# Attention of a macaron block: exponentials times values as seven block products instead of eight

## The chip, the cores and the metric

The kernel runs on one core of a Trainium2 chip. The metric is the device time of one execution in microseconds (us), as the median of several runs. The engines of the core work in parallel, each with its own queue of instructions: TensorE (PE in the profile; its weight loads are PEld), VectorE (DVE), ScalarE (ACT), GpSimd (POOL), and SyncE (SP), which issues transfers. An engine carries out its queue in order; an instruction that needs another engine's result waits for it, and everything behind it on that engine waits too.

## The reference

The input x has 4 batches of 512 rows and 256 columns, in float32. Three steps follow each other, each on the layernormed x and added to x:

```python
x = x + 0.5 * _L0_ffn_ref(_layernorm(x), ...)
x = x + _L0_attn_ref(_layernorm(x), Wq, Wk, Wv, fc_w, fc_b)
x = x + 0.5 * _L0_ffn_ref(_layernorm(x), ...)      # the same weights
```

The feed-forward part has one shared expert and 16 routed experts, of which each row uses the two with the highest scores. The attention has three heads, each 256 wide:

```python
scores = jnp.einsum('bne,hde->hbnd', x, Wq) ... * scale      # Q K^T
w = jax.nn.softmax(scores, axis=2)            # over the query rows
attn = jnp.einsum('hbnm,hbmd->hbnd', w, V)
return jnp.mean(attn, axis=0) @ fc_w.T + fc_b
```

The softmax runs over the rows n of the queries, so its sum z belongs to a key m and can be moved into the values: V[m] is scaled by 1/z[m]. The mean over heads and the output matrix are folded into the value weights, so the result of attention is the sum over three heads of (exponentials, 512x512) times (values, 512x256).

## The kernel before

**Layout.** A batch of x is a tile xs[b] of 128 partitions x 4 row tiles (index j) x 256 columns. The exponentials es[h] lie with the key on the partitions, as 128 x 4 key tiles (m) x 512 queries; the values vs[h] as 128 x 4 key tiles (m) x 256. All of this is float32, and each float32 matmul shows in the trace as two pairs of a weight load and a matmul.

**One batch of attention** (the loop at L844). GpSimd forms four sums of quarters of the transposed rows (S1 to S4, L855 to L858). query(h) multiplies the rows by a folded matrix on PE (py, 128x512, L868) and ScalarE copies the result to y (L872). quadrants(h) computes the 512x512 scores of a head from seven products of blocks: GpSimd forms the right sums T1 to T4 (L881 to L884), PE multiplies (psc, L896), and ScalarE (L910, L912), GpSimd (L913) and VectorE (L911 to L920) add the parts into ex; VectorE finds the maxima (nmax, L903) and ScalarE takes the exponentials in place (L905), with their sums z. After three heads GpSimd adds the bias to x (L950). value(h) (L924 to L938) multiplies the rows by the folded value weights (pv, L929), and the result is scaled by 1/z on its way out of PSUM: by VectorE for head 1 (L934), by ScalarE for the others (L938). Then the next batch's rows are normalized and transposed (layernorm_T, L261 to L294). The last step is the one that changes: for each row tile j, 12 matmuls over three heads and four key tiles sum into one PSUM bank pa (L970), 256 columns wide, and VectorE adds the bank to x (L975).

**What runs beside it.** For b > 0, the second feed-forward part of the batch before is prepared between the transposes and the products: PE computes the router's scores psr (L335), ScalarE a sigmoid (L353), and then router (L359 to L445) is a chain of small VectorE operations: key (L384), and twice a maximum, comparisons and a mask "one" (L388 to L392), the first followed by L394. PE counts ranks from the masks (psk, L400, in two groups, one after each mask), and the chain goes on on VectorE up to L433. Then GpSimd issues eight indirect transfers (L438), which scatter rows, with their weights in an extra column, to a table in device memory, sorted by expert. After batch 3 and its router, the tail is a series: table, loads, and the routed experts (L628 to L671), whose rows return to x at the very end.

**Order.** A planner lays the instructions of each engine in an order from the program order and its own costs and due times; a few groups of PE and ScalarE are ordered by hand with in_turn (L814 to L825, L990, L1046), none of them within the batch loop. At the start of batch 2, ffn.more() (L708 to L711) puts a branch that every engine passes; PE then waits for VectorE's queue to have passed it. Pools of tiles set limits as well: PSUM banks come from the tags mm and dn (three each), rt and rk (one each). In SBUF, "ey" has eight buffers, "h" and "g" two each, "xt" three. The tag ey is used by T1, T2 and T4; g by S1 to S4.

Of the kernel before, what the change touches and what calls it, by code (L numbers as in the profile page):

```python
# [10 lines left out]
F32 = mybir.dt.float32  # L11
# [4 lines left out]
ALU = mybir.AluOpType  # L16
AX = mybir.AxisListType
P = 128
# [3 lines left out]
def tile_macaron_block(  # L22
# [33 lines left out]
    nc = tc.nc  # L56
    B, N, H = x.shape
    NH = Wq.shape[0]
    NE = gate_w.shape[1]
    F = shared_gate_w.shape[1]  # L60
    NJ = N // P
# [37 lines left out]
    work = ctx.enter_context(tc.tile_pool(name="work", bufs=2))  # L99
    att = ctx.enter_context(tc.tile_pool(name="att", bufs=2))  # L100
    dram = ctx.enter_context(tc.tile_pool(name="dram", bufs=1, space=bass.MemoryType.DRAM))
    psum = ctx.enter_context(tc.tile_pool(name="psum", bufs=3, space=bass.MemoryType.PSUM))
# [25 lines left out]
    xs = []  # L128
# [113 lines left out]
    def moments(b, n, on_act=False):  # L242

        mv = small.tile([P, NJ, 2], F32, tag="mv", name=f"mv_{n}")
        for j in range(NJ):
            st = small.tile([P, 6], F32, tag="st", name=f"st_{n}_{j}")
            nc.vector.bn_stats(out=st, in_=xs[b][:, j, :])
            nc.vector.bn_aggr(out=mv[:, j, :], in_=st)
        std = small.tile([P, NJ], F32, tag="std", name=f"std_{n}")
        rooted[n] = mark(f"root {n}", nc.scalar.activation(std, mv[:, :, 1], AF.Sqrt, bias=eps))  # L250
        rstd = small.tile([P, NJ], F32, tag="rstd", name=f"rstd_{n}")
        last = nc.vector.reciprocal(rstd, std)
        off = None
        if on_act:
            off = small.tile([P, NJ], F32, tag="off", name=f"off_{n}")
            last = nc.vector.scalar_tensor_tensor(
                off, mv[:, :, 0], -1.0, rstd, ALU.mult, ALU.mult
            )
        return mv, rstd, off, last

    def layernorm_T(b, which, dispatch=False, moms=None):  # L261

        n = f"{which}_{b}"
        mv, rstd, off, _ = moms or moments(b, n)

        pts = [psum.tile([P, N], F32, tag="dn", name=f"pt_{n}_{c}") for c in range(NC)]
        rows = (
            partial(att.tile, tag="y", bufs=4) if n in ("ln0_2", "ln0_3")
            else partial(work.tile, tag="xn", bufs=4)
        )  # L270
        xn = [rows([P, NJ, W], F32, name=f"xn_{n}_{k}") for k in range(NK if dispatch else 1)]
        for j in range(NJ):
            if off is not None and n != "ln0_1":
                mark(f"norm {n}", nc.scalar.activation(
                    xn[0][:, j, 0:H], xs[b][:, j, :], AF.Identity,
                    bias=off[:, j : j + 1], scale=rstd[:, j : j + 1],
                ))
            else:
                normed[n] = nc.vector.tensor_scalar(
                    xn[0][:, j, 0:H], xs[b][:, j, :], mv[:, j, 0:1], rstd[:, j : j + 1],  # L280
                    ALU.subtract, ALU.mult,
                )
            for c in range(NC):
                mark(f"T{n}", nc.tensor.transpose(  # L284
                    pts[c][:, j * P : (j + 1) * P], xn[0][:, j, c * P : (c + 1) * P], ident
                ))
        xnT = acts.tile([P, NC, N], F32, tag=f"xnT{b}", name=f"xnT_{n}")
        ins = mark(f"copy {n}", nc.scalar.copy(xnT[:, 0, :], pts[0]))
        if off is not None or n == "ln0_0":
            ins = mark(f"copy {n}", nc.scalar.copy(xnT[:, 1, :], pts[1]))  # L290
        else:
            nc.vector.tensor_copy(xnT[:, 1, :], pts[1])  # L292
        copied[n] = ins
        return xnT, xn  # L294
# [443 lines left out]
    m = [moments(0, "ln0_0")]  # L738
# [105 lines left out]
    for b in range(B):  # L844
# [6 lines left out]
        halves = [slice(0, N // 2), slice(N // 2, N)]  # L851
# [9 lines left out]
        ys, es, rzs, vs = {}, {}, {}, {}  # L861
# [62 lines left out]
        def value(h):  # L924
            v = vs[h] = att.tile([P, NJ, H], F32, tag="y", name=f"v_{b}_{h}", bufs=4)
            for m in range(NJ):
                pv = psum.tile([P, H], F32, tag="mm", name=f"pv_{b}_{h}_{m}")
                for c in range(NC):
                    nc.tensor.matmul(  # L929
                        pv, xnT[:, c, m * P : (m + 1) * P], G[h][:, c, :],  # L930
                        start=(c == 0), stop=(c == NC - 1),
                    )
                if h == 1:
                    nc.vector.tensor_scalar(  # L934
                        v[:, m, :], pv, rzs[h][:, m : m + 1], None, ALU.mult
                    )
                else:
                    nc.scalar.mul(v[:, m, :], pv, rzs[h][:, m : m + 1])  # L938
# [9 lines left out]
        quadrants(1)  # L948
        quadrants(2)
        nc.gpsimd.tensor_tensor(xs[b], xs[b], fcb4, ALU.add)  # L950
        for h in range(NH):
            value(h)
        if b + 1 < B:
            ffn.add(b + 1)
            att_xnT[b + 1], _ = layernorm_T(b + 1, "lna")
        if b > 0:
# [4 lines left out]
            if b == B - 1:  # L961
# [1 line left out]
                ffn2.early()  # L963
                ffn2.loads()
                ffn2.empty()
        for j in range(NJ):
            pa = psum.tile([P, H], F32, tag="mm", name=f"pa_{b}_{j}")
            for h in range(NH):
                for m in range(NJ):
                    nc.tensor.matmul(  # L970
                        pa, es[h][:, m, j * P : (j + 1) * P], vs[h][:, m, :],
                        start=(h == 0 and m == 0), stop=(h == NH - 1 and m == NJ - 1),
                    )
            xj = xs[b][:, j, :]
            nc.vector.tensor_tensor(xj, xj, pa, ALU.add)  # L975


    ffn2.scores(B - 1)
# [55 lines left out]
    halves = [slice(j, j + 2) for j in range(0, NJ, 2)]  # L1034
# [44 lines left out]
```

## Time and profile before

| What | Value |
|---|---|
| Median of 3 runs | 508.78 us (508.70 to 510.14) |
| Profiled execution: its time | 540.54 us |
| Profiled execution: its span | 538.7 us |
| Attention of batches 1, 2, 3 in the trace | 220.97 to 286.61, to 352.13, to 416.00 |
| PE busy in the span | 484.5 us (90%) |
| Products exponentials x values on PE | 384 matmuls of 128x256 |
| Adds of the products to x on VectorE (L975) | 16, of 0.42 us |
| Indirect scatters of the routers on GpSimd (L438) | 64, of 0.98 us |

The profiled execution is longer than the median of the runs; durations and sums below are of this one execution. A row of the groups reads: line, engine, operation, output <- inputs, shape, count, then total busy time and mean nanoseconds of one, then the idle time of the engine just before such instructions and what ended most of it. In the timeline each line is the start, the duration, the engine, the line and the operation; a bracket holds the idle time before it and what released it. In the chain in order of time each line is a start, a duration, an engine, the tile and the line: it follows the work that ended last. "PEclk" or the granted clock is TensorE's clock as a share of full speed.

### The profile page before, as it was taken

The numbers are of one execution on the slowest core, as the hardware profiler recorded it, in microseconds if no ns is written. First come the engines' busy times: TensorE is split into PE (matmuls) and PEld (weight loads), VectorE is DVE, ScalarE is ACT, GpSimd is POOL, SyncE is SP. The second block draws the span as 40 slices with busy tenths as digits, with TensorE's granted clock in tenths as the row PEclk, the third lists the DMA queues.
The fourth block names the chain that finished last, engine by engine and source line by source line (L and its number), as shares of the span: only waits on it lengthen the run. The fifth ranks groups of instructions, "written<-read, shape, count | busy, mean of one in ns | idle before, by whom it ended". The sixth has DMA issues, their size and how long they took to land. (4 is left out here: it accounts for less than half of the span.)

```text
span 538.7 us, 7948 instructions
## 1 busy us (share of the span) xinstructions
PE 484.5 (90%) x2262; PEld 374.9 (70%) x2262; DVE 295.4 (55%) x981; ACT 224.6 (42%) x514; POOL 234.7 (44%) x281
## 2 busy tenths in 40 slices
PE   8977249999999899999999999999999767999984
PEld 4666037888656788678885778867888445788852
DVE  6834345555787771258325883336753642555565
ACT  3743015666543770255402664054630313466630
POOL 2466714665658321242254512553014174355653
PEclk9877769999999999999999999999999886999998
DMA  7993364557420000000012000200002245255856
GB/s 266 357 370 125 118 226 122 164 161 230 170 89 1 2 0 1 0 0 2 2 69 89 0 2 0 79 2 1 1 11 99 64 171 178 90 165 179 273 177 208
DMA packets 34734, 57.39 MB, mean 107 GB/s; under 512 B 4928, under 2 KB 25408, under 8 KB 34688
## 3 DMA queue, kind: packets, MB, share of 16 engines
q1 hardware_dynamic: 25424, 32.99, 19.7%
q0 software_dynamic: 8160, 23.44, 12.0%
q10 hardware_dynamic: 1104, 0.42, 0.3%
q8 instruction: 20, 0.33, 0.3%
q14 instruction: 26, 0.21, 0.1%
HBM read 30.78 MB, written 26.05 MB: 105 GB/s over the span
## 5 line engine op out<-in xcount | busy, mean ns | idle before, releaser
L671 POOL DMA_INDIRECT y_d<-ey,to x82 | 80.0, 976 | 66.5 <-ACT xt L632 45.8
L438 POOL DMA_INDIRECT xn_d<-xn_ln,pos x64 | 62.5, 977 | 91.7 <-DVE fa L489 23.0
L644 PE MATMUL peg<-gu,xt 128*128 x328 | 87.5, 391 | 1.9 <-DVE g L597 1.6
L970 PE MATMUL pa<-v,ex 128*128 128x256 f32 x384 | 86.2, 382 | 0.0
L970 PEld LDWEIGHTS pa<-v,ex 128*128 128x128 f32 x384 | 71.6, 190 | 9.2
L644 PEld LDWEIGHTS peg<-gu,xt 128*128 128x128 f32 x328 | 57.6, 195 | 9.0 <-issue 1.7
L661 DVE COPY hT<-pht 128x128 f32<-128x128 f32 x82 | 23.8, 291 | 60.1 <-issue 28.6
L666 PE MATMUL pey<-dn,hT 128*128 x164 | 50.4, 390 | 5.6 <-DVE hT L661 4.6
L670 ACT ACTIVATE ey<-pey,xg 128x256 f32<-128x256 f32 x82 | 38.9, 474 | 28.0 <-issue 15.7
L929 PE MATMUL pv<-G,xnT_lna 128*128 128x256 f32 x192 | 43.5, 382 | 2.7 <-ACT v L938 2.1
L868 PE MATMUL py<-xnT_lna,A 128*128 128x512 f32 x96 | 42.7, 593 | 1.0 <-DVEq L710 1.0
L929 PEld LDWEIGHTS pv<-G,xnT_lna 128*128 128x128 f32 x192 | 36.0, 190 | 9.6 <-ACT v L938 3.3
L905 ACT ACTIVATE ex<-ex,nmax 128x512 f32<-128x512 f32 x48 | 34.2, 714 | 18.6 <-DVE nmax L903 18.4
L650 ACT ACTIVATE sig<-peg 128x128 f32<-128x128 f32 x82 | 22.8, 278 | 42.7 <-PE peg L644 27.3
L632 ACT COPY xt<-pxt 128x256 f32<-128x256 f32 x82 | 29.8, 366 | 14.6 <-PE pxt L628 8.4
L605 PE MATMUL po<-sd,h 128*128 128x256 f32 x64 | 17.1, 415 | 19.1 <-DVE h L598 17.7
L975 DVE TENSOR_TENSOR x<-x,pa 128x256 f32<-128x256 f32 x16 | 6.7, 420 | 50.1 <-PE pa L970 41.3
L666 PEld LDWEIGHTS pey<-dn,hT 128*128 128x128 f32 x164 | 25.2, 194 | 12.4 <-issue 5.1
L628 PE MATMUL pxt<-ident,xg 128*128 128x128 f32 x164 | 32.3, 279 | 0.9 <-DVE xnT_ln L292 0.8
L872 ACT COPY y<-py 128x512 f32<-128x512 f32 x24 | 13.8, 581 | 46.1 <-PE py L868 46.0
L868 PEld LDWEIGHTS py<-xnT_lna,A 128*128 128x128 f32 x96 | 18.2, 190 | 20.6 <-issue 19.8
L881 POOL TENSOR_TENSOR right<-y 128x256 f32<-128x256 f32 x12 | 9.3, 775 | 50.0 <-ACT y L872 50.0
(201 smaller groups left out, 876.0 us busy)
## 6 DMA issues: line engine op xcount, KB each, us to landing
xg<-xn_d SPq DMA_DIRECT2D x82, 129.0 KB
gu<-ffn_experts_gate_up_dram SPq DMA_DIRECT2D x4, 1024.0 KB
yg<-y_d SPq DMA_DIRECT2D x8, 512.0 KB
y<-y_d SPq DMA_DIRECT2D x6, 512.0 KB
dn<-_L_ffn_experts_down_dram SPq DMA_DIRECT2D x2, 1024.0 KB
x<-in_L_attn_x_dram SPq DMA_DIRECT2D x3, 512.0 KB
out_dram<-x SPq DMA_DIRECT2D x3, 512.0 KB
y_d<-ey,to POOLq DMA_INDIRECT x82
```

Of the source, the lines that this page charges most:

```text
L438: ins = nc.gpsimd.indirect_dma_start(out=self.xn_v[k * NT + b * NJ + j], out_offset=bass.IndirectOffsetOnAxis(ap=pos[:, k, j : j + 1], axi ...
L628: ins = nc.tensor.transpose(pt[:, c, :], xg[:, c * P : (c + 1) * P], ident)
L632: nc.scalar.copy(xt, pt)
L644: nc.tensor.matmul(pg, xt[:, c, :], gu[:, bass.ds(e, 1), c, :], start=(c == 0), stop=(c == NC - 1),)
L661: self.flips.append(nc.vector.tensor_copy(hT, pt))
L666: self.downed = nc.tensor.matmul(py, hT, dn[:, bass.ds(e, 1), :], start=True, stop=True)
L670: nc.scalar.mul(y, py, xg[:, H + 1 : W])
L671: ins = nc.gpsimd.indirect_dma_start(out=self.y_v[i], out_offset=bass.IndirectOffsetOnAxis(ap=tos[i], axis=0), in_=y, in_offset=None,)
L868: nc.tensor.matmul(py, A[h][:, c, fc * P : (fc + 1) * P], xnT[:, c, :], start=(c == 0), stop=(c == NC - 1),)
L905: nc.scalar.activation(ex[:, m, :], ex[:, m, :], AF.Exp, bias=nmax[:, m : m + 1], accum_out=z[:, m : m + 1],)
L929: nc.tensor.matmul(pv, xnT[:, c, m * P : (m + 1) * P], G[h][:, c, :], start=(c == 0), stop=(c == NC - 1),)
L970: nc.tensor.matmul(pa, es[h][:, m, j * P : (j + 1) * P], vs[h][:, m, :], start=(h == 0 and m == 0), stop=(h == NH - 1 and m == NJ - 1),)
```

## The change

The exponentials and the values of each head are cut into 2x2 blocks: E11, E21, E12, E22 are halves of the keys (two m each) by halves of the queries, V11, V12, V21, V22 halves of the keys by halves of the columns. The four blocks of the result, x11 to x22, are then formed from seven products of blocks instead of eight. A product is a sum over three heads and two key tiles for two row tiles, in one PSUM bank of 128 x 2 x 128; its matmuls are 128 columns wide.

- GpSimd forms, per head, R1 = E21 + E22 in a new tile (tags h, h and g) and E21 = E11 - E21 in place, 128x512 each.
- VectorE forms, per head, W1 = V12 - V11 and W2 = V22 - W1 in new tiles (tag ey) and V12 = V22 - V12 in place, 128x256 each.
- Between the products VectorE updates the blocks in place: E11 = R1 - E11 after product 1, E12 = E12 - E11 and V21 = W2 - V21 after product 2, each per head.
- The results are added to x part by part. ScalarE copies product 1 to u; VectorE adds products to x11, u, w, x22, x12 and x21; GpSimd adds u to x12 and w to x21 and x22.
- The four matmul groups at L970 and the four adds at L975 are removed.

In the order that the planner makes of it, head 0's two GpSimd sums come among the T sums of head 2, ahead of L913 of head 1; those of heads 1 and 2 come after the last L913. VectorE's updates stand between the router's steps of the same phase. GpSimd's additions of w to x21 and x22 come behind the eight scatters L438 of that phase in batches 1 to 3.

```diff
         quadrants(2)
         nc.gpsimd.tensor_tensor(xs[b], xs[b], fcb4, ALU.add)
+        cols = [slice(0, P), slice(P, H)]
+        E11, E21, E12, E22 = (
+            [es[h][:, m : m + 2, n] for h in range(NH)] for m in (0, 2) for n in halves
+        )
+        R1 = [
+            work.tile([P, 2, N // 2], F32, tag="hhg"[h], name=f"r1_{b}_{h}") for h in range(NH)
+        ]
+        for h in range(NH):
+            nc.gpsimd.tensor_tensor(R1[h], E21[h], E22[h], ALU.add)
+            nc.gpsimd.tensor_tensor(E21[h], E11[h], E21[h], ALU.subtract)
+        V11, V12, V21, V22, W1, W2 = ([] for _ in range(6))
         for h in range(NH):
             value(h)
+            for part, (m, f) in zip((V11, V12, V21, V22), ((m, f) for m in (0, 2) for f in cols)):
+                part.append(vs[h][:, m : m + 2, f])
+            for part in (W1, W2):
+                part.append(work.tile(
+                    [P, 2, P], F32, tag="ey", name=f"w_{b}_{h}_{len(part)}", bufs=8
+                ))
+            nc.vector.tensor_tensor(W1[h], V12[h], V11[h], ALU.subtract)
+            nc.vector.tensor_tensor(W2[h], V22[h], W1[h], ALU.subtract)
+            nc.vector.tensor_tensor(V12[h], V22[h], V12[h], ALU.subtract)
...
-        for j in range(NJ):
-            pa = psum.tile([P, H], F32, tag="mm", name=f"pa_{b}_{j}")
-            for h in range(NH):
-                for m in range(NJ):
-                    nc.tensor.matmul(
-                        pa, es[h][:, m, j * P : (j + 1) * P], vs[h][:, m, :],
-                        start=(h == 0 and m == 0), stop=(h == NH - 1 and m == NJ - 1),
-                    )
-            xj = xs[b][:, j, :]
-            nc.vector.tensor_tensor(xj, xj, pa, ALU.add)
+        x11, x12, x21, x22 = (xs[b][:, j : j + 2, f] for j in (0, 2) for f in cols)
+        def summed(i, lhs, rhs):
+            pa = psum.tile([P, 2, P], F32, tag="mm", name=f"pa_{b}_{i}")
+            for j in range(2):
+                for h in range(NH):
+                    for m in range(2):
+                        nc.tensor.matmul(
+                            pa[:, j, :], lhs[h][:, m, j * P : (j + 1) * P], rhs[h][:, m, :],
+                            start=(h == 0 and m == 0), stop=(h == NH - 1 and m == 1),
+                        )
+            return pa
+        u, w = (work.tile([P, 2, P], F32, tag="xt", name=f"uw_{b}_{i}", bufs=3) for i in range(2))
+        p1 = summed(1, E11, V11)
+        nc.scalar.copy(u, p1)
+        nc.vector.tensor_tensor(x11, x11, p1, ALU.add)
+        for h in range(NH):
+            nc.vector.tensor_tensor(E11[h], R1[h], E11[h], ALU.subtract)
+        p2 = summed(2, E12, V21)
+        nc.vector.tensor_tensor(x11, x11, p2, ALU.add)
+        for h in range(NH):
+            nc.vector.tensor_tensor(E12[h], E12[h], E11[h], ALU.subtract)
+            nc.vector.tensor_tensor(V21[h], W2[h], V21[h], ALU.subtract)
+        p6 = summed(6, E11, W2)
+        nc.vector.tensor_tensor(u, u, p6, ALU.add)
+        p7 = summed(7, E21, V12)
+        nc.vector.tensor_tensor(w, u, p7, ALU.add)
+        nc.gpsimd.tensor_tensor(x12, x12, u, ALU.add)
+        p5 = summed(5, R1, W1)
+        nc.vector.tensor_tensor(x22, x22, p5, ALU.add)
+        nc.vector.tensor_tensor(x12, x12, p5, ALU.add)
+        nc.gpsimd.tensor_tensor(x21, x21, w, ALU.add)
+        nc.gpsimd.tensor_tensor(x22, x22, w, ALU.add)
+        p4 = summed(4, E22, V21)
+        nc.vector.tensor_tensor(x21, x21, p4, ALU.subtract)
+        p3 = summed(3, E12, V22)
+        nc.vector.tensor_tensor(x12, x12, p3, ALU.add)
```

## The prediction

> **What bounds the kernel now.** I read busy shares, a windows view cut at the batches' borders, groups, the chain in order of time, and the timeline around batch 1's products, in that order.
>
> ```profile
> PE 484.5 (90%) x2262; PEld 374.9 (70%) x2262; DVE 295.4 (55%) x981; ACT 224.6 (42%) x514; POOL 234.7 (44%) x281
> ```
>
> TensorE has work for 90% of the span. By stage (start:end, length, busy time of PE, PEld, DVE, ACT, POOL, then the granted clock):
>
> ```profile
> core 0: us, PE busy (x) PEld busy (x) DVE busy (x) ACT busy (x) POOL busy (x), PEclk, DMA share, GB/s
> 220.97:286.61 65.64, 63.98 (x295) 51.49 (x294) 31.12 (x68) 24.49 (x51) 23.02 (x27) 1.00 0.06 21
> 286.61:352.13 65.52, 64.46 (x293) 51.48 (x294) 39.42 (x94) 27.00 (x54) 26.27 (x32) 1.00 0.08 29
> 352.13:416.00 63.87, 63.21 (x290) 50.79 (x289) 35.13 (x96) 26.17 (x52) 20.48 (x25) 1.00 0.06 20
> 437.50:447.40 9.90, 3.92 (x11) 2.14 (x11) 1.00 (x5) 1.12 (x3) 6.13 (x7) 0.61 0.65 254
> 447.40:456.00 8.60, 8.60 (x30) 6.69 (x31) 3.05 (x15) 3.92 (x12) 3.86 (x4) 0.66 0.43 125
> ```
>
> The first three rows are attention of batches 1 to 3: PE fills them to 97-99% at full clock, the other engines have half of the time free. So cutting PE's work could pay there 1:1, and any new wait of PE costs 1:1. The last two rows are the entry to the routed experts: PE idles, and the next stretch still has clock 0.66.
>
> ```profile
> L970 PE MATMUL pa<-v,ex 128*128 128x256 f32 x384 | 86.2, 382 | 0.0
> ...
> L913 POOL TENSOR_TENSOR ex<-ex 128x512 f32<-128x512 f32 x12 | 15.2, 1270 | 11.4 <-ACT ex L912 11.4
> ```
>
> The products to be changed are 384 instruction pairs, 96 per batch. A mean of 382 overlaps its neighbours, so I take the pitch from the chain below: 68 pairs in 14.76 us, 217 ns each, 20.8 us a batch. The chain, batch 2:
>
> ```profile
> 309.19 1.23 POOL ex L913
> ...
> 310.44 0.70 DVE ex L915
> ...
> 337.33 14.76 PE pa L970 x68
> ```
>
> Before the values, the chain leaves PE for GpSimd's add L913 and a run of VectorE steps to the last exponential; lateness on GpSimd there is lateness of PE. After it the products run unbroken. Batch 1's end, timeline:
>
> ```profile
> 265.94 0.23 DVE L384 TENSOR_TENSOR key<-s,bias_bc 128x64 f32<-128x64 f32 x1 [2.19 <-ACT s L353]
> ...
> 267.23 0.23 DVE L392 TENSOR_TENSOR one<-rev,first 128x64 bf16<-128x64 f32 x1
> ...
> 281.43 0.97 POOL L438 DMA_INDIRECT xn_d<-xn_ln,pos  x1 [0.30 <-issue]
> ...
> 285.58 0.42 DVE L975 TENSOR_TENSOR x<-x,pa 128x256 f32<-128x256 f32 x1 [4.76 <-PE psk L400]
> ...
> 286.61 0.67 PE L868 MATMUL py<-xnT_lna,A 128*128 128x512 f32 x1 [1.01 <-DVEq L710]
> ```
>
> Three things run beside the products: the router's chain on VectorE (L384 to L433), eight row scatters on GpSimd (272.46 to 282.40, pitch 1.28), and the adds L975. Nothing after L975 waits for the scatters now. Batch 2's first query matmul waits for VectorE's queue to pass the branch at L710.
>
> **TensorE.** Removed per batch: 96 pairs at 256 columns. Added: 7 x 2 x 3 x 2 x 2 = 168 pairs at 128 columns. Near rows: transposes with 128 columns, 8 in 0.87 us = 109 ns; psr (16 columns, the same weights) 14 in 1.47 = 105. I take 110: 18.5 us against 20.8, -2.35 per batch, -9.4 in all. Break-even is 124 ns. Against this speaks the Trainium skill ("TensorE: Matmul & The Clock Gate", section "Back-to-back issue gap"): sustained weight-load-and-matmul pairs of 128 columns take some 81 ns where the isolated matmul takes 56, because the weight load shares the budget. That ratio, 1.46, on my 110 gives an estimate of 160 ns, 26.9 us a batch, +24 over four. The transposes alternate both operands too and stay at 109, so I keep 110; 160 is the upper end.
>
> **Sums ahead of the products.** GpSimd gets six 128x512 sums per batch, 6 x 1.27 = 7.6 us. By the changed program's order, head 0's second sum stands ahead of L913 of head 1, so that L913, VectorE's chain, the values and PE come 1.25 later. The rest lies behind the last L913, under values and transposes. VectorE gets nine 128x256 operations (0.42 each, L975); three stand before the evictions L934 that PE's value banks wait for: +0.5, in batch 0 up to +1.0. Together about +1.75 (b0 +2.2). An operation delayed[...] is seen once (an L732 add of 1024 columns took 2.19 instead of 1.45), but L913 runs beside VectorE's maxima unslowed: 0 to +1 a batch, I take 0.2.
>
> **VectorE among the products.** Removed: four L975 adds (1.7). Added: nine 128x512 updates in place (0.70, L915) and eight half-size adds to x, u, w (0.42 each): 6.3 + 3.4 = 9.7. They stand between the router's steps in VectorE's queue. The first needs product 1, and key (L384) stands behind two of them. Batch 1, with the phase 1.75 later: the router's scores (psr) end at 267.25 instead of 265.5; each product is 24 pairs, 2.64 us, and product 1 ends near 268.8, since some of its pairs fill gaps between the transposes and scores as the pairs do now; two updates, then key ends 269.8 (was 266.2). Until the first "one" mask there are then x11, a third update, E12 of head 0 and V21 of head 0 (2.5 us): 273.4 (was 267.5). PE's rank matmuls (L400) wait for it within product 6, a stall of 1.4. Up to the second mask lie x11, the other four updates and u: 278.0 (was 270.4), a stall of 1.3 within product 7. Product 7 ends at 279.8, and 5, 4, 3 end at 282.45, 285.1, 287.7. PE alone ends so 2.2 later than now: the saving is spent on the stalls.
>
> **GpSimd's queue.** The pair of adds x21+=w, x22+=w stands behind the eight scatters in GpSimd's order. The scatters start after the router's tail: 272.46 + 7.6 = 280.05, last end 290.0. Then x21+=w to 291.0 (0.73 by the 128x256 rows of L881-L884). VectorE's x21-=p4 must follow it, x12+=p3 comes behind that: 291.9. Queued behind these on VectorE is the branch L710, so py starts at 292.5 instead of 286.61: **+5.9**, with PE idle for 4.8. Batch 0 has no router in its products: +2.2 - 2.35 = **-0.1**. Batch 2: the same gate; x21-=p4 holds the bank of product 4, which the second query tile of batch 3 needs: 358.9 instead of 352.97, **+5.9**, and +0.5 because the fetch of the next rows and GpSimd's next sums come behind it. Batch 3: scatters 411 to 421.2, x21 at 421.95, x22 at 422.7; x12+=p3 and then four row statistics of x (one remained before) to the root at 424.95 against 417.12: +7.8, and +0.5 for the second router's start behind it: **+8.3**. The tail (norm, scores, scatters, experts) is serial after it and takes it 1:1.
>
> **Clock.** The trace has PE busy 3.92 of 9.90 at 437.5, then 0.61 and 0.66. The Trainium skill (same page, "The HAM clock gate") says that idleness throttles the array and that some us of work release it. By the rows alone, an idle time of 5 to 8 us costs nothing beyond itself or up to 8.60 x 0.34 = 2.9; three gaps, 0 to 8.7. I take 2.5 in all: only 4.8 us are empty in the first gap, and the third runs into a serial tail, where the clock matters little.
>
> **Sum.** -0.1 + 5.9 + 6.4 + 8.3 + 2.5 = +23.0, on the profiled execution's 540.54 (span 538.7). The runs' median, 508.78, is 6% under it, though the attention part has clock 1.00 in the profile; waits for GpSimd don't scale with TensorE's clock. I take +22: 508.8 + 22 = **531**.
>
> **Rivals.**
> A. *The gate is weak*: scatters overlap, VectorE catches up, and only the insertion on GpSimd and the rank stalls count, about +2 to +3 per batch: 508.8 + 10 = 519. For it: x21+=w itself needs only product 7. Against it: the queue order is fixed.
> B. *PE is the bound and the rest is hidden* (the other side): below 124 ns a pair, with no wait for the scatters: -9.4 gives 499.4; with the delay ahead of the values (3 x 1.75 + 2.2 = 7.45) it is 506.8, still faster. It decides only if the scatters end before product 4 does (285.1), so if they start 5 us sooner than I work out. For it: 97-99% of PE. Against it: scatters ended at 282.4 even before, and the router is now behind 9 us of updates.
> C. *No net change*: B's gain meets A's costs: 508.8.
> D. *Narrow pairs are dear*: 160 ns adds 24 on PE; longer products hide about half of the gate, +35: 544. Serial (load and stream one after the other, 216) would give about 577. Against it: 109 in the transposes.
>
> **How the numbers follow.** Chances: main case 0.72, A 0.10, B 0.07, C 0.03, D 0.08. The main case's own range: the gates' sum 20.5 less 4 (the router's delay over-counted by 1.3 a batch) gives 525; clock and port at their upper ends, +8.7 + 4 - 3, give 540. The range reaches to A's middle below and D's estimate above: 515 to 545, with some 0.08 below and 0.06 above it. About 0.3% is what a measurement of this kernel can tell from no change. Faster by more: B, and a little of A, 0.08. Within: 0.03. Slower: 0.89.
>
> **What would show it.** Right: 168 pairs at about 110 ns where unbroken; L913 of head 1 later by 1.25; the first mask 4 to 6 us later against the scores; scatters right ahead of x21+=w on GpSimd; the query of batch 2 released by VectorE's queue, with 4 to 6 us of idle PE; the last statistics held by GpSimd's x22. Wrong: if scatters start soon after the scores (VectorE takes router steps between the updates without waiting), the gate shrinks; if pairs take over 124 ns, PE is the bound and slower; if GpSimd's adds slow down beside VectorE's updates, the sum is too small.

## The result

The changed kernel takes 528.26 us (median of 4 runs, 527.37 to 528.58) against 509.46 for the kernel before: 1.0356 times as long, 95% interval 1.0327 to 1.0385, that is 3.6% or some 18.8 us slower. The forecast was 531, or +22.

The first part of the page of the changed kernel, to be set against the row shown of before:

```profile
PE 482.5 (92%) x2549; PEld 377.8 (72%) x2550; DVE 336.0 (64%) x1069; ACT 225.4 (43%) x518; POOL 274.9 (52%) x317
```

TensorE has 287 instructions more; VectorE has 41 us more work, GpSimd 40 us more. This profiled execution took 528.58 (span 526.8), close to its median, while the first profiled execution of the kernel before had been 540.54. Busy times of TensorE from the two are not comparable, so the kernel before was profiled once more:

> The kernel before, unchanged, for a second profiled execution. The first one was 540.5 against a median of 508.8. If the attention part is stable, batch 1 to batch 2 and batch 2 to batch 3 take 65.6 and 65.5 again from first query to first query, and the 30 us lie in the two feed-forward parts; if not, the stage sums of my comparison are off by what differs.

It took 509.02 (span 507.2), with this row:

```profile
PE 475.9 (94%) x2261; PEld 370.6 (73%) x2262; DVE 294.5 (58%) x981; ACT 224.5 (44%) x514; POOL 234.3 (46%) x281
```

Against it TensorE is busy for 6.6 us more after the change, not for less. Its windows, batch by batch from the first query matmul to the next one, then to the reciprocal L252 of batch 3's norm, then to the first scatter of the last router (columns as in the windows shown of before):

```profile
135.66:200.73 65.07, 62.90 (x269) 49.89 (x268) 38.48 (x74) 26.89 (x52) 24.23 (x25) 1.00 0.02 7
200.73:266.37 65.64, 63.98 (x296) 51.49 (x294) 31.12 (x68) 24.50 (x51) 22.97 (x27) 1.00 0.06 19
266.37:331.67 65.30, 64.24 (x293) 51.28 (x293) 39.38 (x93) 26.99 (x54) 26.51 (x32) 1.00 0.08 31
331.67:397.19 65.52, 64.86 (x294) 51.36 (x292) 36.14 (x99) 26.49 (x54) 20.44 (x25) 1.00 0.07 23
397.19:407.91 10.72, 7.68 (x50) 5.34 (x49) 6.91 (x31) 4.65 (x9) 0.00 (x1) 1.00 0.30 76
```

Batches 1 and 2 take 65.64 and 65.30, as in the first profile (65.64 and 65.52). Nearly all of the 31.5 us between the two executions lie in the feed-forward parts: attention began at 155.9 there and begins at 135.7 here, and the part after the last router's first scatter is 10 us shorter here. The same windows of the changed kernel:

```profile
135.88:201.58 65.70, 61.74 (x341) 50.27 (x340) 49.67 (x90) 25.86 (x52) 34.31 (x33) 1.00 0.02 7
201.58:271.56 69.98, 63.52 (x368) 51.88 (x367) 42.74 (x96) 25.90 (x53) 32.30 (x37) 1.00 0.05 16
271.56:338.75 67.19, 65.01 (x364) 52.41 (x365) 47.09 (x108) 26.09 (x54) 32.70 (x35) 0.98 0.08 27
338.75:411.94 73.19, 64.94 (x367) 51.54 (x365) 46.86 (x128) 28.38 (x56) 34.82 (x41) 0.99 0.07 23
411.94:426.85 14.91, 12.48 (x49) 9.11 (x49) 7.01 (x31) 4.38 (x8) 0.00 (x0) 0.57 0.27 71
```

| Stage | Before (second profile) | After | Difference | Forecast |
|---|---|---|---|---|
| Batch 0 | 65.07 | 65.70 | +0.6 | -0.1 |
| Batch 1 | 65.64 | 69.98 | +4.3 | +5.9 |
| Batch 2 | 65.30 | 67.19 | +1.9 | } +14.7 |
| Batch 3, to L252 | 65.52 | 73.19 | +7.7 | } for both |
| L252 to the last router's first scatter | 10.72 | 14.91 | +4.2 | clock, +2.5 for all gaps |
| Rest (to the span's end) | 99.3 | 99.95 | +0.7 | 0 |
| Sum | | | +19.4 | +23.0 |

In the first two rows of after PE is busy for up to 1.2 us less than before, and in batch 1 it stands idle for 6.5 us instead of 1.7. In the last row the granted clock is 0.57, and PE is busy for 12.48 us with the work that took 7.68 before: 4.8 of the 6.6 us are this stretch.

**The gate.** The end of batch 1 in the timeline of the changed kernel:

```profile
258.89 2.84 PE L997 MATMUL pa<-w,r 128*128 128x128 f32 x24
...
259.37 1.00 POOL L438 DMA_INDIRECT xn_d<-xn_ln,pos  x1 [1.58 <-DVE xn_ln L433]
...
261.57 5.52 PE L997 MATMUL pa<-v,ex 128*128 128x128 f32 x48
...
268.33 0.97 POOL L438 DMA_INDIRECT xn_d<-xn_ln,pos  x1 [0.30 <-issue]
269.32 0.73 POOL L1022 TENSOR_TENSOR x<-x,uw 128x256 f32<-128x256 f32 x1
...
270.09 0.42 DVE L1025 TENSOR_TENSOR x<-x,pa 128x256 f32<-128x256 f32 x1 [7.57 <-POOL x L1022]
...
271.56 1.19 PE L868 MATMUL py<-xnT_lna,A 128*128 128x512 f32 x1 [4.42 <-DVEq L710]
```

Read it from the end. The query waits 4.42 us for VectorE's queue; VectorE stood 7.57 us in L1025 for GpSimd's L1022; L1022 starts as soon as the eighth scatter has been issued. PE had finished product 3 by 267.1. This wait of TensorE for GpSimd's queue, by way of VectorE's, is called the gate below. The first two PE lines also price the narrow pair: 24 pairs from 258.89 to 261.57, 111.7 ns each.

**Ahead of the values.** GpSimd and VectorE in the middle of batch 1:

```profile
220.53 1.31 POOL L961 TENSOR_TENSOR r<-ex 128x512 f32<-128x512 f32 x1 [6.78 <-ACT ex L905]
221.79 0.73 POOL L881 TENSOR_TENSOR right<-y 128x256 f32<-128x256 f32 x1
...
222.48 1.27 POOL L962 TENSOR_TENSOR ex<-ex 128x512 f32<-128x512 f32 x1
...
225.76 1.26 POOL L913 TENSOR_TENSOR ex<-ex 128x512 f32<-128x512 f32 x1
227.05 0.69 DVE L915 TENSOR_TENSOR ex<-ex,psc 128x512 f32<-128x512 f32 x1 [3.64 <-POOL ex L913]
```

Both sums of head 0 (L961, L962) stand ahead of L913 of head 1, not one. L913 starts 24.18 after the batch's first query; in the second profile of the kernel before it starts at 222.44, 21.71 after it. VectorE waits 3.64 for it. The scatters begin at 259.37, 57.79 after the first query, instead of 51.49.

### The profile page after: what moved, and what is told of

Its sections match the earlier page's. It is cut to its first block, busy times and chain, and to the rows that moved or that the text cites. A ratio compares the mean times of both kernels' runs of the same rounds, so it can differ in the third digit from the quotient of the medians.

```text
span 526.8 us, 8711 instructions
## 1 busy us (share of the span) xinstructions
PE 482.5 (92%) x2549; PEld 377.8 (72%) x2550; DVE 336.0 (64%) x1069; ACT 225.4 (43%) x518; POOL 274.9 (52%) x317
## 5 line engine op out<-in xcount | busy, mean ns | idle before, releaser
L438 POOL DMA_INDIRECT xn_d<-xn_ln,pos x64 | 62.3, 974 | 54.4 <-DVE held L459 17.1
L997 PE MATMUL pa<-v,ex 128*128 128x128 f32 x480 | 57.9, 277 | 0.0
L997 PEld LDWEIGHTS pa<-v,ex 128*128 128x128 f32 x480 | 55.5, 192 | 0.1
L666 PE MATMUL pey<-dn,hT 128*128 x164 | 49.3, 383 | 1.4 <-DVE hT L661 1.4
L868 PE MATMUL py<-xnT_lna,A 128*128 128x512 f32 x96 | 44.5, 611 | 6.1 <-DVEq L710 4.4
L929 PE MATMUL pv<-G,xnT_lna 128*128 128x256 f32 x192 | 45.1, 385 | 3.9 <-ACT v L938 2.3
L872 ACT COPY y<-py 128x512 f32<-128x512 f32 x24 | 13.7, 579 | 80.1 <-PE py L868 80.1
L961 POOL TENSOR_TENSOR r<-ex 128x512 f32<-128x512 f32 x12 | 15.6, 1302 | 56.7 <-ACT ex L905 56.7
L868 PEld LDWEIGHTS py<-xnT_lna,A 128*128 128x128 f32 x96 | 18.6, 197 | 26.8 <-issue 23.1
L628 PEld LDWEIGHTS pxt<-ident,xg 128*128 128x128 f32 x164 | 22.9, 144 | 12.8 <-DMA xg<-xn_d 2.0
L903 DVE TENSOR_REDUCE nmax<-ex 128x2 f32<-128x1024 f32 x24 | 29.1, 1213 | 0.1
## 6 DMA issues: line engine op xcount, KB each, us to landing
gu<-ffn_experts_gate_up_dram SPq DMA_DIRECT2D x4, 1024.0 KB, 14.7
```

The costliest lines, as they stand in the source:

```text
L438: ins = nc.gpsimd.indirect_dma_start(out=self.xn_v[k * NT + b * NJ + j], out_offset=bass.IndirectOffsetOnAxis(ap=pos[:, k, j : j + 1], axi ...
L628: ins = nc.tensor.transpose(pt[:, c, :], xg[:, c * P : (c + 1) * P], ident)
L666: self.downed = nc.tensor.matmul(py, hT, dn[:, bass.ds(e, 1), :], start=True, stop=True)
L868: nc.tensor.matmul(py, A[h][:, c, fc * P : (fc + 1) * P], xnT[:, c, :], start=(c == 0), stop=(c == NC - 1),)
L903: nc.vector.tensor_reduce(nmax[:, ms], ex[:, ms, :], AX.X, ALU.max, negate=True)
L929: nc.tensor.matmul(pv, xnT[:, c, m * P : (m + 1) * P], G[h][:, c, :], start=(c == 0), stop=(c == NC - 1),)
```

## Experiments

My theory: the change pays 2 us a batch on TensorE and loses it by three separate waits, (a) GpSimd's sums ahead of L913, (b) the router delayed on VectorE, (c) the additions of w behind the scatters, and by the half clock that follows the gaps (the stretches of granted clock near 0.5). Rivals: narrow pairs are dear; or the additional work as such fills the engines, so that no single wait matters. All ratios are to the kernel before; the changed kernel stands at 1.0356.

### The narrow pair alone

```diff
-            for h in range(NH):
-                for m in range(NJ):
-                    nc.tensor.matmul(
-                        pa, es[h][:, m, j * P : (j + 1) * P], vs[h][:, m, :],
...
+            for f in (slice(0, P), slice(P, H)):
+                for h in range(NH):
+                    for m in range(NJ):
+                        nc.tensor.matmul(
+                            pa[:, f], es[h][:, m, j * P : (j + 1) * P], vs[h][:, m, f],
```

> The kernel before with its eight block products, each row tile's group cut into two column halves: 192 pairs of 128 columns per batch instead of 96 of 256, nothing else. If a 128-column pair takes the 111.5 ns that 24 of them take in the changed kernel (2.68 us from product 5 to product 4), the products take 21.4 us a batch instead of 20.8: +0.6 a batch, about +2.3 in all, 511 to 512. If narrow pairs were dear in this place (rival D, 160 ns), 30.7 us a batch and about 548.

Measured: 513.38, ratio 1.0045 (1.0019 to 1.0072), some 2.3 us. Narrow pairs cost what the changed kernel's own trace says; rival D is out. The change's 168 pairs at 111.7 ns take 18.8 us, so 2.1 less than 96 wide ones.

### The additions of w on VectorE

```diff
-        nc.gpsimd.tensor_tensor(x21, x21, w, ALU.add)
-        nc.gpsimd.tensor_tensor(x22, x22, w, ALU.add)
+        nc.vector.tensor_tensor(x21, x21, w, ALU.add)
+        nc.vector.tensor_tensor(x22, x22, w, ALU.add)
```

> The changed kernel with its two additions of w to x21 and x22 on VectorE instead of GpSimd, so that nothing of x stands behind the scatters. My theory (the gate): the idle 4.4 us of TensorE before batch 2 fall to 1, batch 3's second query tile no longer waits (2.7), batch 3's statistics come 3 earlier, and the half clock after these gaps goes (1.6 and about 3): about -12, so 516, range 513 to 519. Rival A (lateness ahead of the values and of the router is what counts): under -4, so 525 or more.

Measured: 523.94, ratio 1.0234 (1.0190 to 1.0279). The gain is real (the interval does not touch the changed kernel's), but the time lies between the two expectations. Batch 1 takes 66.98 instead of 69.98, as the theory has it. Batch 2 shows where the rest went, timeline of this run:

```profile
269.56 0.97 POOL L438 DMA_INDIRECT xn_d<-xn_ln,pos  x1 [0.30 <-issue]
269.76 7.11 PE L868 MATMUL py<-xnT_lna,A 128*128 128x512 f32 x16 [1.40 <-DVEq L710]
...
273.39 0.80 SPq L720 DMA_DIRECT2D yg<-y_d  x2
...
277.10 2.89 DVE L732 TENSOR_TENSOR x<-x,yg 128x1024 f32<-128x1024 f32 x2 [8.33 <-DMA yg<-y_d]
...
283.44 3.70 PE L868 MATMUL py<-xnT_lna,A 128*128 128x512 f32 x8 [0.53 <-DVE ex L911]
```

PE starts batch 2 at once, but the scatters are still late, and by the code the fetch of the next batch's rows takes buffers of the tag xn, from which the scatters read: it is issued 3.6 after the first query (in the first profile of before at 284.93, 1.7 ahead of it). The rows are then added and normalized by VectorE in front of batch 2's score additions. So batch 2 takes 68.53 instead of 67.19: the lateness of the scatters has a second way to PE. The tail's half clock stayed too: the 12 us from 408 on have a mean granted clock of 0.57.

### GpSimd's sums behind the last L913

```diff
-            nc.gpsimd.tensor_tensor(C11, C11, C21, ALU.add)
+            l913[b, h] = nc.gpsimd.tensor_tensor(C11, C11, C21, ALU.add)
...
         for h in range(NH):
-            nc.gpsimd.tensor_tensor(R1[h], E21[h], E22[h], ALU.add)
-            nc.gpsimd.tensor_tensor(E21[h], E11[h], E21[h], ALU.subtract)
+            with tc.issue_after(l913[b, NH - 1].ins):
+                nc.gpsimd.tensor_tensor(R1[h], E21[h], E22[h], ALU.add)
+                nc.gpsimd.tensor_tensor(E21[h], E11[h], E21[h], ALU.subtract)
```

> The changed kernel with all six GpSimd sums of a batch behind head 2's L913; the additions of w stay behind the scatters. By the trace both sums of head 0, not one, stand ahead of L913 of head 1. My theory: L913 of head 1 comes 2.5 us earlier in batches 1 to 3 (its start against the batch's first query as before, 21.7), the scatters and all behind them with it, so -2 to -2.5 a batch in three batches and less in batch 0: about -7, so 521. If the chain there has slack, or the sums come too late for product 7: 527 to 530.

Measured: 520.96, ratio 1.0205 (1.0161 to 1.0249), as the theory has it. GpSimd in batch 1 of this run (first query at 199.96):

```profile
222.24 1.27 POOL L913 TENSOR_TENSOR ex<-ex 128x512 f32<-128x512 f32 x1
...
225.81 1.27 POOL L913 TENSOR_TENSOR ex<-ex 128x512 f32<-128x512 f32 x1 [2.29 <-ACT ex L912]
227.03 1.31 POOL L961 TENSOR_TENSOR r<-ex 128x512 f32<-128x512 f32 x1
```

Head 1's L913 is at 22.28 from the query (24.18 in the changed kernel, 21.71 in the kernel before), the scatters begin 1.8 earlier against it, and the gate is as wide as in the changed kernel (PE waits 4.41 for L710). Batch 0, which has no router, falls to 63.73, 1.3 under the kernel before: there the product's saving comes through.

### Both edits together

> Both single edits together: GpSimd's six sums behind the last L913, and the additions of w on VectorE. If the two costs are separate, the gains add: 7.3 + 4.3 from 528.3 gives 516.7. If the earlier scatters already make the gate cheaper, or the sums fall where the gate was, 519 or more.

Measured: 515.75, ratio 1.0101 (1.0067 to 1.0135). The two costs are separate: 1.5 and 1.2 points make 2.7, and 2.6 are measured. Of the 5 us that remain, some 3.4 stand in the stretch from L252 to the last router's first scatter: 14.07 us instead of 10.72, at a mean granted clock of 0.64.

### The router ahead of the updates

The products in another order, so that four of them need none of VectorE's updates:

```diff
+        p1 = summed(1, E11, V11)
+        nc.scalar.copy(u, p1)
+        nc.vector.tensor_tensor(x11, x11, p1, ALU.add)
+        p2 = summed(2, E12, V21)
+        nc.vector.tensor_tensor(x11, x11, p2, ALU.add)
+        nc.gpsimd.tensor_tensor(x12, x12, u, ALU.add)
+        p7 = summed(7, E21, V12)
+        nc.vector.tensor_tensor(w, u, p7, ALU.add)
+        p5 = summed(5, R1, W1)
...
+        with ExitStack() as behind_router:
+            if b > 0:
+                behind_router.enter_context(tc.issue_after(ffn2.last.ins))
+            for h in range(NH):
+                nc.vector.tensor_tensor(E11[h], R1[h], E11[h], ALU.subtract)
+            for h in range(NH):
+                nc.vector.tensor_tensor(E12[h], E12[h], E11[h], ALU.subtract)
+                nc.vector.tensor_tensor(V21[h], W2[h], V21[h], ALU.subtract)
+        p6 = summed(6, E11, W2)
+        nc.vector.tensor_tensor(w, w, p6, ALU.add)
+        nc.vector.tensor_tensor(x12, x12, p6, ALU.add)
```

> The changed kernel with the products in the order 1, 2, 7, 5, 6, 4, 3 and the updates of E11, E12 and V21 behind the router's last step on VectorE (the same number of operations; x12 takes product 6 and the copy of product 1 apart). The additions of w stay on GpSimd behind the scatters. My theory: the router's delay of 3.7 us against the phase goes, the scatters end before product 4 does, so the gate shrinks to under 1 us without moving the additions: about -10, so 518, range 515 to 521. Rival: the gate waits for the scatters wherever they are, or product 6 now waits for late updates: 524 or more.

Measured: 526.91, ratio 1.0331 (1.0275 to 1.0387): no gain that can be told from none. My expectation missed. Timeline of batch 1's end in this run:

```profile
250.46 0.42 DVE L1006 TENSOR_TENSOR x<-x,pa 128x256 f32<-128x256 f32 x1 [1.33 <-ACT uw L1005]
...
256.01 1.27 POOL L438 DMA_INDIRECT xn_d<-xn_ln,pos  x1 [4.78 <-DVE xn_ln L433]
257.59 1.20 POOL L438 DMA_INDIRECT xn_d<-xn_ln,pos  x1 [0.30 <-issue]
...
267.06 0.73 POOL L857 TENSOR_TENSOR left<-xnT_lna 128x256 f32<-128x256 f32 x1
...
269.18 0.42 DVE L1029 TENSOR_TENSOR x<-x,pa 128x256 f32<-128x256 f32 x1 [6.76 <-POOL x L1026]
```

The scatters do begin 2.8 earlier against the batch's first query (54.98 instead of 57.79). Three things take it back: the addition of product 1 to x11 still makes VectorE wait 1.33 in the middle of the router; the first four scatters, now beside the updates, come every 1.5 to 1.6 us instead of 1.28; and the planner has put S3 and S4 (L857, L858) ahead of both additions of w, 1.4 us more of gate. PE still waits 3.62 us for L710. Batch 1 takes 69.62 instead of 69.98, batch 2 68.85 instead of 67.19, batch 3 73.76 instead of 73.19. So delaying the router less does not help while the additions stay behind the scatters.

### The same additions, only ahead of the scatters

The eight scatters of batches 1 to 3 are held back and issued behind x22+=w, and so behind S3 and S4, which stand ahead of it; in batch 3 the loads of the expert tables move behind them:

```diff
+        w22 = nc.gpsimd.tensor_tensor(x22, x22, w, ALU.add)
+        if b > 0:
+            with tc.issue_after(w22.ins):
+                ffn2.scatter()
```

> The changed kernel with the same work on the same engines, and only GpSimd's order changed: the eight scatters of batches 1 to 3 behind x21+=w, S3, S4 and x22+=w instead of ahead of them. If the order is what makes the wait, batch 2's first query comes 66.5 to 67.5 after batch 1's (69.98 in the changed kernel), as with the additions on VectorE, and batch 3's second query tile waits no more; but the scatters end some 5 later, the fetch of the next rows with them, so the total is 522 to 526. If only taking work off GpSimd helped, it stays at 528.

Measured: 533.32, ratio 1.0428 (1.0380 to 1.0476). One half of the expectation held: batch 2's first query comes 66.91 after batch 1's, so the gate is GpSimd's order and not the work. The total missed; batch 2 takes 73.29. Timeline (the lines are shifted by four in this kernel: L724 is L720, L736 is L732, L872 is L868):

```profile
279.02 0.80 SPq L724 DMA_DIRECT2D yg<-y_d  x2
...
282.85 3.11 DVE L736 TENSOR_TENSOR x<-x,yg 128x1024 f32<-128x1024 f32 x2 [12.80 <-DMA yg<-y_d]
...
289.41 1.13 PE L872 MATMUL py<-xnT_lna,A 128*128 128x512 f32 x2 [3.54 <-DVE ex L915]
```

The scatters end at 276.5, the fetch goes out 8 us after the first query, and VectorE waits 12.80 us for its rows with batch 2's score additions queued behind. The second way of the scatters to PE, seen faintly above, is the wider one here.

### The half clock in the tail

```diff
+    busy = psum.tile([P, 2, P], F32, tag="mm", name="busy")
+    for i in range(18):
+        nc.tensor.matmul(busy[:, 0, :], E22[0][:, 0, 0:P], V22[0][:, 0, :], start=(i == 0), stop=(i == 17))
     ffn2.scores(B - 1)
```

> The changed kernel with 18 more float32 matmuls of 128 columns behind batch 3's last product, whose sum nobody reads: some 4 us of work for TensorE in the gap of 4.7 us in which it waits for batch 3's statistics. If the idle time causes the half clock from 412 to 424 in the changed kernel, the clock stays up and the time from the reciprocal L252 to the first scatter falls from 14.9 to 11 or 12, and the total by some 2 to 3, to 525 to 526.5. If the clock falls for another reason, nothing changes, or 0.5 is lost: 528 to 529.

Measured: 526.76, ratio 1.0341 (1.0302 to 1.0380), not to be told from the changed kernel. Windows of the changed kernel over its gap and the 12 us behind it, then of this run:

```profile
406.00:412.00 6.00, 1.88 (x6) 0.57 (x4) 2.57 (x11) 2.18 (x3) 3.44 (x5) 0.93 0.27 88
412.00:424.00 12.00, 11.02 (x37) 8.16 (x38) 5.45 (x20) 3.73 (x6) 0.00 (x0) 0.50 0.34 89
```

```profile
402.00:409.00 7.00, 7.00 (x65) 7.00 (x64) 0.24 (x2) 0.00 (x0) 5.45 (x7) 1.00 0.28 97
409.00:421.00 12.00, 8.89 (x47) 6.01 (x47) 5.72 (x21) 4.48 (x8) 1.06 (x3) 0.91 0.42 111
```

With the gap filled, the clock is 0.91 instead of 0.50 in the windows shown: the idle time has to do with it. But the way from L252 to the last router's first scatter falls only from 14.91 to 13.58, and not to 11 or 12: the router's scores now wait 1.80 for ScalarE's copy of the transposed rows (L288), and the clock falls to 0.50 behind that wait, from 420 to 422. How much of the 4.2 us is the clock's can be read from the run with the router ahead, above, in whose profiled execution the clock did not fall. The same stretch there:

```profile
413.32:424.14 10.82, 7.54 (x49) 5.22 (x49) 6.91 (x31) 4.14 (x8) 0.06 (x1) 1.00 0.28 73
```

It takes 10.82 at clock 1.00, as long as in the kernel before (10.72), and PE is busy for 7.54 with the 49 instructions that take 12.48 in the changed kernel. So nearly all of the 4.2 us is the clock's. Whether the clock falls is not a matter of the gap's length alone: PE had stood idle for 2.96 us ahead of this stretch, and the same 2.96 us were followed by 0.64 in the run with everything together, below.

### Everything together, and without batch 3

Sums late, additions on VectorE, the router ahead (with both additions to x11 behind it as well), and S3 and S4 in buffers of the tag ey:

> Everything together: sums behind the last L913, additions of w on VectorE, products in the order 1, 2, 7, 5, 6, 4, 3 with all VectorE updates and the two x11 additions behind the router's last step, and S3 and S4 in buffers of another tag, so that they need not wait for product 5. If the waits named so far are all that the change costs, each of batches 1 to 3 takes 64 to 65.5 from query to query, and the time is 504 to 511. If something else bounds it (the four statistics after the last product, the late fetch), 513 or more.

Measured: 516.99, ratio 1.0119 (1.0077 to 1.0160). Batches 0 to 2 take 64.05, 64.94 and 64.45, all under the kernel before, and within what was expected; batch 3 misses it with 70.39 to L252, and the tail takes 14.22. In batch 3 VectorE also works out the expert tables, and the timeline has

```profile
384.36 2.94 PE L997 MATMUL pa<-w,r 128*128 128x128 f32 x24 [0.58 <-DVE uw L1009]
...
389.05 2.65 PE L997 MATMUL pa<-w,ex 128*128 128x128 f32 x20 [0.88 <-DVE ex L1019]
...
401.18 0.18 DVE L252 RECIPROCAL rstd_ln<-std_ln 128x4 f32<-128x4 f32 x1 [1.75 <-ACT std_ln L250]
401.87 0.33 PE L284 MATMUL pt_ln<-ident,xn_ln 128*128 128x128 f32 x1 [2.96 <-DVE xn_ln L279]
```

PE waits for late additions and updates, and then 2.96 for the norm, which cannot start before the last product: every row tile gets a part of its sum late, so all four statistics follow it. The last of them ends at 399.43, but the root L250 starts only at 400.85, because ScalarE stands in L591 (0.60) and in a load of its table (1.28) ahead of it; in the kernel before, L250's load ran early, while ScalarE was idle. Against the two edits alone (65.14, 66.64 and 67.78 for batches 1 to 3, the last to L252), the router's order and the buffers of S3 and S4 win 0.2 in batch 1 and 2.2 in batch 2, and lose 2.6 in batch 3. Cost (b), the delayed router, is thus not shown to have a part of its own in the 18.8 us. That led to the version with seven products in batches 0 to 2 and the old eight in batch 3:

```diff
+        seven = b < B - 1
...
+        for h in range(NH) if seven else ():
...
+        for j in range(0 if seven else NJ):
```

> The four moves together in batches 0 to 2, and batch 3 with the eight products of the kernel before. In four_moves batches 0 to 2 took 64.05, 64.94 and 64.45 from query to query against 65.07, 65.64 and 65.30 in the kernel before: -2.6; batch 3 and the tail should be as before. So 0.995 of the kernel before, 506 to 507.5. If batch 2's gain was only lent (its scatters and fetch come back in batch 3), no difference: 509.

Measured: 507.76 (12 runs), ratio 0.9957 (0.9936 to 0.9978). It is faster than both kernels, than the kernel before by 0.4%. Its windows:

```profile
135.54:200.00 64.46, 62.48 (x342) 51.82 (x340) 52.99 (x93) 25.74 (x52) 32.64 (x31) 0.97 0.02 8
200.00:264.94 64.94, 62.63 (x369) 52.15 (x367) 45.07 (x99) 25.89 (x53) 31.18 (x33) 1.00 0.05 17
264.94:329.44 64.50, 62.81 (x364) 51.93 (x365) 50.13 (x112) 26.30 (x54) 38.01 (x40) 1.00 0.10 34
329.44:396.47 67.03, 65.61 (x295) 51.12 (x293) 38.21 (x104) 27.42 (x55) 20.50 (x26) 1.00 0.07 22
```

The three changed batches win 0.6, 0.7 and 0.8; the fourth, with its old products, loses 1.5 of these 2.1 again in this execution. By the trace its loss comes from the batch before it, whose rows are complete only after the last product: the reciprocal L252 of their norm starts 4.21 after batch 3's first query instead of 1.66 (four statistics stand between, where one did, and the table load of 1.28 again), ScalarE's copies L346 and L466 follow later, its last copy of y (L872), which comes behind them, starts at 9.07 instead of 7.07, and head 0's L913 at 11.85 instead of 10.32. The batch keeps these 1.5 us up to the router's scores. That the moved buffers of S3 and S4 bring the gain without the seven products was not tested; PE's busy time in the three windows is 0.4, 1.3 and 1.4 less than in the kernel before, which speaks for the products.

## Why the prediction was right

**TensorE.** Forecast 110 ns a pair and -2.35 a batch; measured 111.7 ns and -2.1. The ratio of the Trainium skill ("TensorE: Matmul & The Clock Gate", section "Back-to-back issue gap") that I carried over to these float32 pairs, 160 ns as an estimate, is not borne out: the row of the transposes was the right neighbour.

**Sums ahead of the products.** The step was under-sized. I counted one sum of head 0 ahead of L913; the first one stands ahead of head 2's T sums too, so both count: 2.47, not 1.25. The three VectorE operations ahead of the evictions cost next to nothing instead of 0.5: the last 14 matmuls of the router's scores begin 2.64 later against the first query (45.68 instead of 43.04), 0.2 more than L913. So the step's sum is 2.64 in batch 1 where 1.75 was forecast. Moving the sums gave 1.5 points of the ratio, some 7.7 us, more than any other single edit.

**VectorE among the products.** The direction was right, the size too large. The scatters begin 57.79 after batch 1's first query instead of 51.49, +6.3, of which 2.6 come from the phase: 3.7 are the router's own, not 5.85. I had added durations, but on VectorE the next operation starts earlier than that, 0.13 after this router step of 0.22 and 0.60 after this update of 0.68:

```profile
251.37 0.22 DVE L388 TENSOR_REDUCE top<-key 128x4 f32<-128x64 f32 x1
251.50 0.68 DVE L1008 TENSOR_TENSOR ex<-r,ex 128x512 f32<-128x512 f32 x1
252.10 0.22 DVE L389 TENSOR_TENSOR eq<-key,top 128x64 f32<-128x64 f32 x1
```

The two rank stalls of 1.4 and 1.3 on PE are not in the trace at all.

**GpSimd's queue.** The mechanism is shown: the order of queue entries sets it (moving the same work ahead of the scatters freed the first query of batch 2), and its cost in place is 1.2 points of the ratio, 6 us. In batch 1 PE is idle for 4.4 where 4.8 was forecast. The steps for batches 2 and 3 were too large: together +9.6 instead of +14.7, of which 1.5 are the clock's (below). The scatters begin 6.9 later against the first query in batch 2, where the forecast had 7.6, and 9.5 later in batch 3, but there 3.3 of it stand already at head 0's L913; of their own these are some 6.2, where the forecast had 9.0. That the late scatters also hold the fetch was in the forecast at 0.5; with scatters later still it becomes the larger wait.

**Clock.** Forecast +2.5, less than half of what came. Two gaps are followed by a lower clock: batch 2's first 16 query matmuls take 8.62 instead of 7.11, 1.5 more, and the tail's stretch takes 4.2 more, nearly all the clock's. That makes 5.6. The reason I gave for the low term, that the third gap runs into a serial tail where the clock matters little, was wrong: it mattered most there, where the same 49 instructions of TensorE took 12.48 us instead of 7.54.

**Sum.** +23 on paper, +22 taken, +18.8 measured. The mechanism was the one forecast, but that the total came so near is in part luck: batches 1 to 3, sums and gates together and without the clock, were put some 8 us too high, the clock 3 us too low, batch 0 and the rest 1.4 us too low, and these errors go opposite ways. Rival A's weak gate and B's hidden one are excluded by PE's 4.42 us at L710, C, equal times, by the interval, and D by the narrow pairs alone. Yet B's core, that products can pay if nothing waits, is what the last version shows at 0.4%.

## What to carry to other kernels

A cheaper product on the busy engine pays only if its extra sums find queue places that nobody behind them waits for. Ask, of each added operation, which queue it enters, ahead of what, and behind what: here the same two additions cost 6 us behind eight scatters, and the same two sums some 8 us ahead of one addition. A result that is completed in pieces also delays whatever needs a whole row of it, which is why the last batch, with a serial tail behind it, did better with the old form here. And when TensorE comes to wait, ask what a lower clock behind the wait would cost: here it was some 5.6 of 18.8 us.

## What the runs showed of the hardware that I had not expected

VectorE operations with two SBUF inputs were slowed by GpSimd's sums more than I allowed. The timeline of batch 1 of the changed kernel, VectorE and then GpSimd:

```profile
240.41 1.42 DVE L972 TENSOR_TENSOR w<-v 128x256 f32<-128x256 f32 x1
...
243.50 0.41 DVE L972 TENSOR_TENSOR w<-v 128x256 f32<-128x256 f32 x1
```

```profile
240.26 1.29 POOL L961 TENSOR_TENSOR r<-ex 128x512 f32<-128x512 f32 x1 [3.40 <-ACT ex L905]
```

L972 takes 0.41 alone and 1.42 at 240.41, where it starts 0.15 after L961 and ends 0.28 behind it. Its 12 instances have a mean of 751 ns, so L972 alone lost some 1.0 us a batch where I took 0.2 for all operations. The Trainium skill ("SBUF — State Buffer", section "SBUF: two separate sides") says of such a VectorE operation and a GpSimd one that reads SBUF that whichever starts first holds a shared port as an exclusive lock for the whole instruction; this row agrees. It stayed off the path, since PE ran on from 239.68 to 244.27 with the products of values. The scatters beside the updates, every 1.5 to 1.6 us instead of 1.28, may have the same cause; no run here shows it.

The half clock lasted much longer than the gap that preceded it: 0.50 through 12 us in which PE was busy for 11.02, after 4.7 us of idleness. The Trainium skill ("TensorE: Matmul & The Clock Gate", section "Part 1: The HAM clock gate (the "warmup" mystery)") gives about 3.4 us of sustained work until the clock is back; this row does not agree, since PE was busy without a break in the last 8 of these 12 us, and no run here shows what kind of work would have been enough after the gap.
